# Transforms along a row as four 64x64 quarters of the array instead of block-diagonal pairs

## Chip, cores and metric

The kernel runs on one core of a Trainium2 chip. The metric is the device time of one execution in microseconds, and a program is judged by the median of several runs.

## What is computed

A 48 x 48 image with 768 channels passes through four layers, one after the other: a transformer block with relative-position attention and an MLP, a spectral layer, a scan layer (a recurrence of 12 steps with a 3x3 convolution), and a second spectral layer. The change concerns the spectral layers and the output of the scan layer. Cut to what matters, a spectral layer is

```python
xs = jnp.fft.rfft2(x, axes=(1, 2))               # rows h, then 25 frequencies along w
# per frequency and block of 96 channels: complex 96x96 layer, relu, complex 96x96 layer
o1 = relu(complex_mul(xs, w1) + b1)
o2 = complex_mul(o1, w2) + b2
out = jnp.fft.irfft2(softshrink(o2, 0.01), s=(48, 48), axes=(1, 2)) + x
```

and the scan layer ends with `silu(h @ W_out + b_out)`. All numbers are 32-bit floats.

## The kernel before

The two-dimensional transform is made as two products with small cosine and sine matrices. The channels are worked in two halves of 384 (`TB`), and the 24 pairs of image rows (two rows of 48 points, 96 partitions) in six groups of four pairs.

**Forward along w** is `spectrum_rows`. One product takes a pair of rows: the stationary matrix `fw` is 96 x 112 and block-diagonal, one block of cosines and sines for each of the two rows, and the 384 channels of the half are the moving columns. A group has four such products, each into a PSUM tile of its own. ScalarE and VectorE empty the tiles in turn (`Evac`, lines 63 and 65), and one DMA writes the group to `yu`, a spectrum in DRAM of 112 lines (frequency, real or imaginary part, row of the pair) by 24 pairs.

**Mixing** is `spectrum_mix`. For each half, each of five chunks of five frequencies, and each of four blocks of 96 channels it runs a software pipeline of four stages: the transform along h (L1559), the first complex layer (L1573 to L1575), the second (L1594, L1595) and the transform back along h (L1609). It loads `yt` from `yu` and stores `us` back into the same places. Other work is put into its steps by a function `beside`.

**Back along w** exists in two forms. In layer 1 (`afno_first`, L1696) the spectrum is the stationary operand and `iw` the moving one, because the scan layer needs channels on partitions. In layer 3 (`afno_second`, L1792) `iw`, 100 x 96 and block-diagonal, is stationary and 384 channels move; VectorE adds the product to `x3` (L1794), and one DMA on ScalarE's queue stores a group of four pairs (L1798). The last group is stored pair by pair on two queues (L1796). The group's spectrum, `gt`, is loaded by one DMA on SyncE's queue (L1784).

Where this work stands:

- The forward transforms of layer 1 run inside the MLP (`afno_follow`). Of twelve groups eleven are put between the MLP's products (L960, L1023), with a PSUM pool of only two tiles; the twelfth runs in the mix of layer 1, with eight.
- The forward transforms of layer 3 run inside the output of the scan layer. There, L1365 makes two rows' 384 output channels, VectorE adds the bias into a temporary `st` (L1367), and ScalarE writes Silu of it into `x3` (L1368), which has 96 partitions by 24 pairs by 768 channels. Every two pairs of row pairs the generator yields, and `afno_second` puts a forward group in (records `so_f`). Both share a pool of six PSUM tiles.
- Of the twelve groups back of layer 3, the six of half 0 are put into the steps of the mix (the table `backs`), and those of half 1 come after its end. For half 1 the lines of the first four chunks are loaded early (`most`), and the lines of the last chunk when its `us` has been stored (`rest`).

The order on each engine is that of the program, as a scheduler of the framework settles it when the kernel is built; each engine then works its list in order and waits on semaphores. The constants are made in `shape_constants`.

Of the kernel before, what the change touches and what calls it, by code (L numbers as in the profile page):

```python
# [20 lines left out]
P = 128  # L21
# [24 lines left out]
YR = 112  # L46
# [1047 lines left out]
def scan_phase(tc, ident, w, wts, rows_back, xh, x_close, c_d, cr_d, out_open):  # L1094
# [18 lines left out]
    K = 112  # L1113
# [5 lines left out]
    with tc.tile_pool(name="sc_s", bufs=1, side="left") as sp:  # L1119
# [3 lines left out]
        def out_weights():  # L1123
            wp = out_open("so_w")
            wo = wp.tile([P, 2, C], F32, tag="wo", name="wo")
            nc.sync.dma_start(wo, wo_d)
            return wo, load_bcast(nc, wp, bo_d, C, "bo", parts=BS)
# [203 lines left out]
        x3 = out_open("x3").tile([BS, NPR, C], F32, tag="x3", name="x3")  # L1331
        hg = s[ITERS % 2].rearrange("p n r t -> p (n r t)").rearrange("p (t n) -> p t n", t=NPR)
        with (
# [11 lines left out]
            def turned(j, q4):  # L1345
# [4 lines left out]
                hTs[j, q4] = tp.tile([P, 4, 2, G], F32, tag=f"hT{j}_{q4}", name=f"hT_{j}_{q4}", bufs=1)  # L1350
                nc.scalar.copy(hTs[j, q4], ps.rearrange("p (i s w) -> p i s w", i=4, s=2)[:, :, :, :G])
# [4 lines left out]
            for half in range(2):  # L1356
                cols = slice(half * TB, (half + 1) * TB)
                for p2 in range(NPR // 2):
                    if half == 0 and p2 % 2 == 0:
                        turned(1, p2 // 2)  # L1360
                    for t in range(2):
                        pr = 2 * p2 + t
                        ps = psum(f"{pr}_{half}")
                        for j in range(2):
                            nc.tensor.matmul(ps[:BS, :TB], lhsT=hTs[j, pr // 4][:, pr % 4].rearrange("p s w -> p (s w)"), rhs=wo[:, j, cols], start=j == 0, stop=j == 1)  # L1365
                        t_ = tp.tile([BS, TB], F32, tag="t", name=f"st_{pr}_{half}")
                        V.tensor_tensor(t_, ps[:BS, :TB], bo[:, cols], ALU.add)  # L1367
                        nc.scalar.activation(x3[:, pr, cols], t_, AF.Silu)  # L1368
# [16 lines left out]
def block_kernel(ctx: ExitStack, tc: tile.TileContext, a: dict):  # L1385
# [68 lines left out]
    yu = [dram.tile([YR, G // 2, TB], F32, tag=f"yu{i}", name=f"yu{i}") for i in range(2)]  # L1454
    todo = []
    follow_in = lambda *args: afno_follow(nc, xa_d, a["fw2"], yu, todo, *args)
# [29 lines left out]

def spectrum_rows(nc, fw, x, yu, half, g, psum, pool, ev, name, bufs=2):

    ys = pool.tile([YR, 4, TB], F32, tag="ys", name=f"{name}_ys_{half}_{g}", bufs=bufs)
    for i in range(4):
        ps = psum(f"f_{half}_{g}_{i}")
        nc.tensor.matmul(ps[:YR, :TB], lhsT=fw, rhs=x[:, i, :], start=True, stop=True)
        ev(ys[:, i, :], ps[:YR, :TB])
    nc.sync.dma_start(yu[half][:, 4 * g : 4 * g + 4, :], ys)


def spectrum_open(tc, stack, name, a, layer, yu, side):  # L1500
# [20 lines left out]
    def load(half, kc):  # L1521
        if (half, kc) not in yts:
            yts[half, kc] = yp.tile([BS, KC, TB], F32, tag="yt", name=f"{name}_yt_{half}_{kc}")
            nc.sync.dma_start(yts[half, kc], yu[half][4 * KC * kc : 4 * KC * (kc + 1)].rearrange("(k q) p c -> (q p) k c", q=4))
# [5 lines left out]
def spectrum_mix(tc, name, opened, yu, psum, keep, side, halves, beside):  # L1530
# [10 lines left out]
    with tc.tile_pool(name=f"{name}_s", bufs=2, side=side) as sp:  # L1541
# [61 lines left out]
        def s_ifft_h(i):  # L1603
# [12 lines left out]
            if b == HB - 1 or (last and b == HB // 2 - 1):  # L1616
                done = slice(b // 2 * 2 * BS, (b + 1) * BS) if last else slice(0, TB)
                nc.sync.dma_start(yu[half][4 * KC * kc : 4 * KC * (kc + 1), :, done].rearrange("(k q) p c -> (q p) k c", q=4), us[:, :, done])
# [11 lines left out]
def load_spectrum(nc, pool, yu, half, g, name, bufs):  # L1630
    gt = pool.tile([YR, 4, TB], F32, tag="gt", name=f"{name}_gt_{half}_{g}", bufs=bufs)
    nc.sync.dma_start(gt, yu[half][:, 4 * g : 4 * g + 4, :])
    return gt


def afno_follow(nc, xa_d, fw_d, yu, todo, pool, bufs=2):

    fw = pool.tile([BS, YR], F32, tag="fw", name="f1_fw")
    nc.sync.dma_start(fw, fw_d)
# [4 lines left out]
    def load(half, g):  # L1644
        cols = slice(half * TB, (half + 1) * TB)
        xt = pool.tile([BS, 4, TB], F32, tag="x1", name=f"f1_x_{half}_{g}", bufs=bufs)
        for s in range(2):
            nc.sync.dma_start(xt[s * G : (s + 1) * G], xv[g, s, :, :, cols])
# [21 lines left out]
def afno_first(tc, a, yu, xh, rp, follow_in, load_next):  # L1670
# [10 lines left out]
    iw = rp.tile([4 * KW, BS], F32, tag="iw", name="f1_iw")  # L1681
# [9 lines left out]
    def back(half, g, dst, psum):  # L1691
        gt = gts.pop((half, g))
        for ct in range(HC):
            ps = psum(f"w_{half}_{g}_{ct}")
            for i in range(4):
                nc.tensor.matmul(ps[:, i * BS : (i + 1) * BS], lhsT=gt[: 4 * KW, i, ct * P : (ct + 1) * P], rhs=iw, start=True, stop=True)  # L1696
            ev(in_rows(dst)[:, ct, :, :G], ps[:, :TB].rearrange("p (h w) -> p h w", w=G))

    with (
# [14 lines left out]
        def beside(step):  # L1714
# [3 lines left out]
            elif step == 8:  # L1718
                nc.sync.dma_start(iw, a["iw"])
# [22 lines left out]
def afno_second(tc, a, scan, yu):  # L1742
# [7 lines left out]
    out = a["out"].rearrange("(p t) c -> t p c", t=BS)  # L1750
    x3, scan_psum = next(scan)
    with ExitStack() as stack:
        opened = spectrum_open(tc, stack, "f3", a, "L3", yu, "right")
        gp = stack.enter_context(tc.tile_pool(name="f3_g", bufs=1, side="right"))
        fw = gp.tile([BS, YR], F32, tag="fw", name="f3_fw")
        nc.sync.dma_start(fw, a["fw2"])
# [178 lines left out]
```

## Time and profile before

| | us |
|---|---|
| median of 3 runs | 3694.07 (3691.95 to 3695.59) |
| profiled execution, its own time | 3694.35 |
| its span | 3692.6 |
| MLP, from 1690 to 2705 us of the span | 1015 |
| mix and back of layer 1, 2705 to 2914 | 209 |
| scan layer, 2914 to 3358 | 444 |
| scan output with forward transform of layer 3, 3358 to 3456 | 98 |
| mix of layer 3 with back of half 0, 3456 to 3660 | 204 |
| end: back of half 1, 3660 to 3693 | 33 |

The profile is that of one execution. Engines: PE is the matrix engine (PEld its weight loads), DVE VectorE, ACT ScalarE, POOL GpSimd, SP SyncE; a q behind a name is the engine's issuing side, DMA issues above all. L1495 is line 1495 of the kernel before. A matmul in 32-bit floats appears as two records. A shape such as 96*112 96x384 is partitions times columns of the stationary operand, then those of the moving one. In the timeline a row is a start, a length, an engine, a line, names of what is written and read, and the number of merged records; the bracket at its end is the idle time before it and what ended it. The end of a matmul record is modelled, so its starts are the better clock.

### The profile page before, as it was taken

Reading aid. Unit: us, or ns where it says so; the run is one execution under the profiler, and the core shown is the slowest. Engines: PE = TensorE matmul, PEld = TensorE weight load, DVE = VectorE, ACT = ScalarE, POOL = GpSimd, SP = SyncE. Lnnn points to the kernel's source line nnn. Section 1 sums busy time; section 2 is a strip of 40 time slices with the busy share of each in tenths; the row PEclk is TensorE's granted clock in tenths of the full one; section 3 lists DMA queues with packets and bytes.
Section 4 is the critical chain, followed back from the end, with each engine's and each line's share of the span. In section 5 each row is a group of like instructions: output and inputs, shape, how many; then the busy total and the mean of one; then the engine's idle time right before and its main releaser. Section 6 shows DMA issues by size and latency. Waiting matters only on the chain.

```text
span 3692.6 us, 52195 instructions
## 1 busy us (share of the span) xinstructions
PE 3592.4 (97%) x20914; PEld 2182.6 (59%) x20914; DVE 1995.3 (54%) x3011; ACT 1140.1 (31%) x1731; POOL 666.3 (18%) x498
## 2 busy tenths in 40 slices
PE   7999989999999999999999999999999998999998
PEld 4666554444444444455555555555568867995685
DVE  6544346666666666655334323232345478994445
ACT  1222134444444444303201210121023265223341
POOL 4010001111111111051000000000023303981131
PEclk9999999999999999999999999999999999999999
DMA  7666764746554543344335433533544302112345
GB/s 254 209 219 191 220 191 127 203 125 160 140 145 118 147 121 102 88 141 157 104 122 171 128 105 121 165 105 107 155 134 111 97 20 101 37 30 83 99 121 154
DMA packets 267738, 491.82 MB, mean 133 GB/s; under 512 B 37182, under 2 KB 220286, under 8 KB 261280
## 3 DMA queue, kind: packets, MB, share of 16 engines
q1 hardware_dynamic: 257680, 467.45, 43.0%
q10 hardware_dynamic: 9808, 20.94, 1.6%
q8 instruction: 168, 2.75, 0.3%
q14 instruction: 82, 0.67, 0.1%
HBM read 344.69 MB, written 143.62 MB: 132 GB/s over the span
## 4 chain that ended last, share of the span: by engine, by line
PE 76%; DVE 3%; POOL 2%; DMA 2%; ACT 1%; issue 1%; ACTq 0%; SPq 0%; DVEq 0%; POOLq 0%
PE p L960 13%; PE p L1023 13%; PE s L623 12%; PE av L654 12%; PE c L1187 4%; PE s L633 3%; PE pj L169 3%; PE f_z L1594 2%; PE f_z L1595 2%; PE f_x L1559 2%; PE so L1365 2%; PE f_u L1609 2%; POOL t L1288 1%; DVE s L1300 1%; DVE H L1284 1%
## 5 line engine op out<-in xcount | busy, mean ns | idle before, releaser
L643 DVE TENSOR_TENSOR acc<-acc,p 128x928 f32<-128x928 f32 (+1 forms) x480 | 565.2, 1177 | 255.2 <-ACT p L635 222.4
L635 ACT ACTIVATE p<-s 128x928 f32<-128x928 f32 (+1 forms) x540 | 506.7, 940 | 522.8 <-PE s L633 501.2
L623 PE MATMUL s<-qt,kv 64*128 64x464 f32 (+1 forms) x2160 | 529.2, 566 | 4.9 <-DMA qt<-q_d 4.9
L1023 PE MATMUL p<-w,h 128*128 128x384 f32 x1512 | 492.7, 486 | 0.0
L654 PE MATMUL av<-p,kv 128*64 128x464 f32 (+1 forms) x2160 | 456.5, 558 | 0.0
L1023 PEld LDWEIGHTS p<-w,h 128*128 128x128 f32 x1512 | 286.2, 190 | 196.9
L633 PE MATMUL s<-bt,oneh 64*128 64x464 f32 (+1 forms) x1080 | 399.1, 729 | 0.9 <-DMA bt<-rh_d 0.9
L623 PEld LDWEIGHTS s<-qt,kv 64*128 64x128 f32 x2160 | 195.4, 187 | 208.0 <-issue 201.7
L960 PE MATMUL p<-x2nT,w 128*128 128x384 f32 x864 | 293.6, 489 | 3.4 <-issue 3.4
L654 PEld LDWEIGHTS av<-p,kv 128*64 128x64 f32 x2160 | 141.9, 137 | 260.5 <-issue 256.7
L355 PE MATMUL qk<-xnT,wqk 128*128 128x384 f32 x756 | 254.0, 493 | 9.2 <-DMA wqk<-wqk_d 9.2
L1280 PE MATMUL c<-H,bands 128*48 128x96 f32 x5632 | 244.0, 247 | 11.4 <-issue 11.0
L1280 PEld LDWEIGHTS c<-H,bands 128*48 128x48 f32 x5632 | 234.4, 123 | 21.2 <-issue 11.4
L960 PEld LDWEIGHTS p<-x2nT,w 128*128 128x128 f32 x864 | 165.3, 191 | 119.3 <-issue 6.0
L960 PE MATMUL p<-xT,w 128*128 128x384 f32 x648 | 220.7, 486 | 0.0
L355 PEld LDWEIGHTS qk<-xnT,wqk 128*128 128x128 f32 x756 | 145.3, 194 | 104.8 <-issue 11.0
L999 POOL TENSOR_TENSOR rr<-rr,ml_b 128x1152 f32<-128x1152 f32 x12 | 33.3, 2776 | 953.6 <-DMA rr<-xr_d 433.0
L955 ACT ACTIVATE h<-h,ml_b 128x384 f32<-128x384 f32 x144 | 88.3, 614 | 346.2 <-DVE h L975 174.3
L1288 POOL TENSOR_TENSOR t<-s,c 128x768 f32<-128x768 f32 x80 | 144.6, 1832 | 182.5 <-DMA bands<-in_bands_dram 171.9
L960 PEld LDWEIGHTS p<-xT,w 128*128 128x128 f32 x648 | 123.1, 190 | 85.9
L633 PEld LDWEIGHTS s<-bt,oneh 64*128 64x128 f32 x1080 | 106.2, 187 | 106.0 <-issue 100.6
L1594 PE MATMUL f_z<-f_w,f_o 97*96 97x96 f32 x800 | 134.5, 250 | 0.0
(323 smaller groups left out, 4677.4 us busy)
## 6 DMA issues: line engine op xcount, KB each, us to landing
w<-w1s_d SPq DMA_DIRECT2D x36, 768.0 KB, 4.2
w<-w2s_d SPq DMA_DIRECT2D x36, 768.0 KB, 4.4
w<-w1s_d SPq DMA_DIRECT2D x36, 576.0 KB, 3.8
w<-in_mlp_w_dram SPq DMA_DIRECT2D x27, 768.0 KB, 4.5
wqk<-wqk_d SPq DMA_DIRECT2D x12, 1344.0 KB, 6.7
yu<-f_ys SPq DMA_DIRECT2D x24, 672.0 KB, 3.8
f_yt<-yu SPq DMA_DIRECT2D x20, 720.0 KB, 6.8
yu<-f_us SPq DMA_DIRECT2D x18, 720.0 KB, 4.5
```

What stands on the lines that cost most here:

```text
L355: nc.tensor.matmul(p[:, :TB], lhsT=w[:, n, c, :], rhs=ops[sb][n][:, c, :], start=c == 0, stop=c == NC2 - 1)
L623: nc.tensor.matmul(ps[:, s, :n], lhsT=keys[pr % 2][rows, kt * P : (kt + 1) * P], rhs=held(c)[rows, :n], start=True, stop=False)
L633: nc.tensor.matmul(ps[:, s, :n], lhsT=oneh[rows, b % 2, :], rhs=bts[b // 2][rows, j, :n], start=False, stop=True)
L635: nc.scalar.activation(p, ps[:, :, :n], AF.Exp)
L643: nc.vector.tensor_tensor(probs[c], probs[c], p, ALU.add)
L654: nc.tensor.matmul(avs[c][rows, : size(c)], lhsT=vals[pr % 2][:, kt, rows], rhs=p[:, s, :], start=kt == 0, stop=kt == NT - 1)
L960: nc.tensor.matmul(p[:, :TB], lhsT=w[n][:, c, :], rhs=rhs[n][:, c, :], start=c == 0, stop=c == NC2 - 1)
L1023: nc.tensor.matmul(ps[t][:, :TB], lhsT=hs[left, f][:, t * P : (t + 1) * P], rhs=wt[:, f % KW2, :], start=f == 0, stop=f == NF2 - 1)
L1187: nc.tensor.matmul(ps[:K, i, :n], lhsT=v[:, c, tok : tok + K], rhs=w[:, cc, c0 : c0 + n], start=cc == NC - 1, stop=cc == 0)
L1280: nc.tensor.matmul(ps[r0 : r0 + G, k // 4, cols], lhsT=bands[:, n - GC, i, :] if gr else bands0[:, n, i, :], rhs=H[:, n, :, d : d + NPR], ...
L1288: GP.tensor_tensor(t, sc[:, ch], c1[:, m0 : m0 + GC].unsqueeze(2).to_broadcast([P, GC, RR, NPR]), ALU.mult)
L1594: nc.tensor.matmul(out, lhsT=o1[:, j, 1:3, :].rearrange("c r h -> c (r h)"), rhs=w2t[:, b, 0, :], start=True, stop=False)
```

## The change

A row of the image gets a 64 x 64 quarter of the array instead of half of a block-diagonal matrix. The operands lie accordingly: two rows at partitions 0 to 47 and 64 to 111, each with its own matrix `fw` (48 x 64) or `iw` (50 x 64) on the same partitions, loaded twice by `by_rows`. In a forward group four quarter products (`a`: partition half of the input row, `b`: partition half of the output) fill two PSUM tiles, and a group has two such sets. Number, place and engine of the evictions stay, now with 128 partitions for 112.

The spectrum in DRAM becomes 64 lines (50 used) by 48 rows; its store and its load take two DMAs per group instead of one, its rows come in another order (the row order of `fh` and `ih` is adapted), and the load in layer 3 takes only the 50 used lines. Layer 1's back transform keeps its form with another constant (`iw2`) and a strided output. In layer 3's back transform four quarter products fill the tiles of two row pairs.

In the scan output, x3 has 112 partitions with a gap between the two rows, so the product has 112 columns, the sum with the bias goes straight into `x3`, and Silu works in place. Each store of the output becomes two. The core of the diff:

```diff
-    ys = pool.tile([YR, 4, TB], F32, tag="ys", name=f"{name}_ys_{half}_{g}", bufs=bufs)
-    for i in range(4):
-        ps = psum(f"f_{half}_{g}_{i}")
-        nc.tensor.matmul(ps[:YR, :TB], lhsT=fw, rhs=x[:, i, :], start=True, stop=True)
-        ev(ys[:, i, :], ps[:YR, :TB])
-    nc.sync.dma_start(yu[half][:, 4 * g : 4 * g + 4, :], ys)
+    ys = pool.tile([P, 2, 2, TB], F32, tag="ys", name=f"{name}_ys_{half}_{g}", bufs=bufs)
+    for j in range(2):
+        ps = [psum(f"f_{half}_{g}_{j}_{a}") for a in range(2)]
+        for a in range(2):
+            keep = slice(a * HD, a * HD + G)
+            for b in range(2):
+                nc.tensor.matmul(ps[a][b * HD : (b + 1) * HD, :TB], lhsT=fw[keep], rhs=x[keep, 2 * j + b, :], start=True, stop=True)
+        for a in range(2):
+            ev(ys[:, j, a, :], ps[a][:, :TB])
+    for b in range(2):
+        nc.sync.dma_start(pairs_of(yu[half], b, g), ys[b * HD : (b + 1) * HD].rearrange("p j a c -> p (j a) c"))
+
+def pairs_of(yu, b, g):
+    n = b * (G // 2) + 4 * g
+    return yu[:, n : n + 4, :]
...
-    yu = [dram.tile([YR, G // 2, TB], F32, tag=f"yu{i}", name=f"yu{i}") for i in range(2)]
+    yu = [dram.tile([HD, G, TB], F32, tag=f"yu{i}", name=f"yu{i}") for i in range(2)]
...
-                nc.tensor.matmul(ps[:, i * BS : (i + 1) * BS], lhsT=gt[: 4 * KW, i, ct * P : (ct + 1) * P], rhs=iw, start=True, stop=True)
+                nc.tensor.matmul(rows[:, i // 2, i % 2], lhsT=gt[:, i, ct * P : (ct + 1) * P], rhs=iw, start=True, stop=True)
...
-                            nc.tensor.matmul(ps[:BS, :TB], lhsT=hTs[j, pr // 4][:, pr % 4].rearrange("p s w -> p (s w)"), rhs=wo[:, j, cols], start=j == 0, stop=j == 1)
-                        t_ = tp.tile([BS, TB], F32, tag="t", name=f"st_{pr}_{half}")
-                        V.tensor_tensor(t_, ps[:BS, :TB], bo[:, cols], ALU.add)
-                        nc.scalar.activation(x3[:, pr, cols], t_, AF.Silu)
+                            nc.tensor.matmul(ps[:K, :TB], lhsT=hTs[j, pr // 4][:, pr % 4], rhs=wo[:, j, cols], start=j == 0, stop=j == 1)
+                        V.tensor_tensor(x3[:, pr, cols], ps[:K, :TB], bo[:, cols], ALU.add)
+                        nc.scalar.activation(x3[:, pr, cols], x3[:, pr, cols], AF.Silu)
...
-            nc.sync.dma_start(gts[half, g][rows], yu[half][rows, 4 * g : 4 * g + 4, :])
+            for b in range(2):
+                nc.sync.dma_start(gts[half, g][b * HD + rows.start : b * HD + rows.stop], pairs_of(yu[half][rows], b, g))
+
+        def store(queue, prs, cols):
+            for s in range(2):
+                queue.dma_start(out[s, :, prs, cols], x3[s * HD : s * HD + G, prs, cols])
...
-            for i in range(4):
-                ps = psum(f"w_{half}_{g}_{i}")
-                nc.tensor.matmul(ps[:BS, :TB], lhsT=iw, rhs=gt[: 4 * KW, i, :], start=True, stop=True)
-                dst = x3[:, 4 * g + i, cols]
-                nc.vector.tensor_tensor(dst, ps[:BS, :TB], dst, ALU.add)
-                if last:
-                    (nc.scalar, nc.sync)[i % 2].dma_start(out[:, 4 * g + i, cols], dst)
+            for j in range(2):
+                ps = [psum(f"w_{half}_{g}_{j}_{b}") for b in range(2)]
+                for b in range(2):
+                    keep = slice(b * HD, b * HD + KR)
+                    for s in range(2):
+                        nc.tensor.matmul(ps[b][s * HD : (s + 1) * HD, :TB], lhsT=iw[keep], rhs=gt[keep, 2 * j + s, :], start=True, stop=True)
+                for b in range(2):
+                    pr = 4 * g + 2 * j + b
+                    dst = x3[:, pr, cols]
+                    nc.vector.tensor_tensor(dst, ps[b][: HD + G, :TB], dst, ALU.add)
+                    if last:
+                        store((nc.scalar, nc.sync)[b], slice(pr, pr + 1), cols)
             if not last:
-                nc.scalar.dma_start(out[:, 4 * g : 4 * g + 4, cols], x3[:, 4 * g : 4 * g + 4, cols])
+                store(nc.scalar, slice(4 * g, 4 * g + 4), cols)
```

When the two programs are built, the scheduler keeps the order of the transforms in the MLP and the scan output: in the MLP the first three products of a group (now the first three tiles) come together, then one matmul of the MLP, then the fourth. It moves a few things elsewhere: loads of `yt` stand later on SyncE's queue, and five products of the scan layer now come before the first back transform of layer 1's second half.

## The prediction

> **What bounds the kernel now.** I read the engine table first, then the windows by stage, then the timeline around each edited line. The page:
>
> ```profile
> PE 3592.4 (97%) x20914; PEld 2182.6 (59%) x20914; DVE 1995.3 (54%) x3011; ACT 1140.1 (31%) x1731; POOL 666.3 (18%) x498
> ```
>
> TensorE is busy 97% of the span, so what leaves its path shortens the run, if no wait takes its place. The stages with edited lines, by windows (columns: length, then busy us of PE, PEld, DVE, ACT, POOL, granted clock, DMA share, GB/s):
>
> ```profile
> 1690.00:2705.00 1015.00, 1015.00 (x3182) 596.08 (x3182) 332.26 (x659) 148.70 (x255) 30.63 (x13) 1.00 0.42 129
> 3358.00:3456.00 98.00, 96.86 (x315) 50.15 (x314) 40.94 (x75) 39.59 (x81) 3.58 (x2) 0.99 0.36 105
> 3600.00:3660.00 60.00, 60.00 (x423) 45.32 (x422) 35.14 (x68) 18.18 (x43) 14.00 (x19) 1.00 0.43 124
> 3660.00:3693.00 33.00, 18.63 (x52) 8.71 (x50) 14.94 (x28) 0.00 (x0) 0.00 (x0) 0.81 0.71 205
> ```
>
> MLP, scan output and the mix of layer 3 are PE from end to end, with DVE and ACT at half or less. The last 33 us are not: loads, PE, DVE and stores follow one another.
>
> How one group of four tiles looks, in the timeline of the scan output and of the MLP:
>
> ```profile
> 3439.04 2.75 PE L1495 MATMUL so_f<-x,f_fw 96*112 96x384 f32 x8
> 3441.62 5.33 PE L1365 MATMUL so<-wo,hT 128*96 128x384 f32 x16
> ...
> 1937.21 2.32 PE L1495 MATMUL f_f<-f_x,f_fw 96*112 96x384 f32 x6
> 1938.63 0.27 PEld L1495 LDWEIGHTS f_f<-f_x,f_fw 96*112 96x112 f32 x2 [0.60 <-ACT f_ys L63]
> ```
>
> A matmul of the program is two records. 3441.62 less 3439.04 is 2.58 us for 8, so 0.322 us each: the price of 384 moving columns. In the MLP the third tile waits for ACT to empty the first (two PSUM tiles there), so a group takes 3.45 us with one MLP matmul (0.645) inside, 2.8 net.
>
> Do tiles of the array run side by side? The attention's `av` uses two 64-column halves in turn:
>
> ```profile
> 1079.73 2.56 PE L654 MATMUL av<-p,kv 128*64 128x464 f32 x12
> ```
>
> One after another, twelve would need 12 x 0.322 x 464/384 = 4.67 us; they take 2.5. The starts of single records come in pairs 7 ns apart, 0.389 us from pair to pair, and the first pair is already one of each half. Two tiles are thus shown; four at once are not.
>
> **What the Trainium skill says.** "TensorE: Matmul & The Clock Gate", Part 3, measures 6.32x for nine and 10.6x for sixteen small tiles at once, a few ns per tile: the pairs agree, no run here shows four. "TensorEngine Tiling (Array Packing)", Key Properties: changing the tiling mode drains TensorE. The trace agrees: the last `av` pair to the next L623 pair is 0.48 us instead of 0.389, and from L203 (96 columns, full array) to L623 0.178 where 96 columns need 0.080. I take 0.10 us a switch. Same page, Gotcha 1: different row tiles need different PSUM banks; the change gives each its own, so no clash is priced in. "DMA: Bandwidth & Descriptors", How many engines: a load spreads over the largest k up to 16 that divides its outer size. So 112, 80 and 32 lines use 16 engines, the new 50, 40 and 10 lines use 10; the trace has no such load to check on.
>
> **The change, part by part.** A group keeps its four PSUM tiles and four evictions; its four matmuls (8 records) become eight quarter matmuls (16 records). If four quarters run together, that is 16/4 x 0.322 = 1.29 us plus two switches, 0.20: 1.49 instead of 2.58, a gain of 1.09 where PE is the path.
>
> 1. Scan output, so_f, 12 groups. The cover: between two groups run 5.16 us of L1365. A group needs rows that ended 2.58 us earlier; the chain from their last record is 0.56 to the DVE start, 0.55, 0.04, ACT 0.52, 0.05 = 1.72. DVE has 4 x 0.55 + 2 x 0.56 = 3.3 and ACT about 3.6 of the new period of 6.65, so neither becomes the bound. Eleven groups gain 12.0; after the twelfth the mix waits for the last evictions (PE starts 3.89 us after its first record), of which I give 1.2. **-13.2**. Writing x3 directly and Silu in place, 112 rows for 96, 112 weight columns for 96 and the hT copy of 448 elements for 384 (0.48 to about 0.53) hide under PE; uncovered they would cost under 0.1 us each.
>
> 2. Layer 3 back, half 0, six groups inside the PE-bound mix (2.58 each): 6 x 1.09 = **-6.5**. Of the step's 6.1 us, DVE uses 4.6. The output store becomes two issues on ACT's queue (0.32 each, waiting for the four adds); behind it stands the copy of L1578, which in the trace follows 2.4 us later. No charge.
>
> 3. MLP, eleven groups. Tiles one and two now stream together, but the third still waits for the first's eviction: switch 0.10, second record at 0.42, ACT from 0.985 (0.564 after the record, as in the trace) to 1.46, third tile 1.51 to 2.25 (with the 0.1 of a cold restart), switch, MLP matmul to 3.0, switch, fourth tile 3.1 to 3.74 on a half-used array, switch: 3.84 against 3.45. **+0.39 x 11 = +4.3**. With free switches it is zero, with 0.15 each +6.5. The transform moves to quarters, but the wait replaces the stream. The store that follows becomes two on SP (0.31 each) and starts about 0.4 later; behind it stand weight loads with four buffers, some 20 us ahead.
>
> 4. Layer 1's last group in the mix, eight banks: 2.60 to 1.49, **-1.1**.
>
> 5. Handovers through DRAM. From MLP to mix, PE's idle 1.5 us at 2705.5 follows the yu store and yt load: one more issue plus item 3's lateness, **+0.7**. The spectrum loads at 2914 become pairs (+0.35), but the scheduler now puts five scan products that don't need them first: 0, between -1 and +1. The yt and us transfers move the same 96 rows of 1536 B; the order of yt_1 and yt_2 behind xa_d and f_x leaves over 10 us to their use. The inverse of layer 1 (L1696) keeps its matmuls and only strides its output: 0.
>
> 6. The end. Now:
>
> ```profile
> 3670.08 17.44 PE L1792 MATMUL f_w<-f_gt,f_iw 100*96 100x384 f32 x48 [8.90 <-DMA f_gt<-yu]
> 3674.01 14.10 DVE L1794 TENSOR_TENSOR x<-f_w,x 96x384 f32<-96x384 f32 x22 [0.50 <-PE f_w L1792]
> ```
>
> PE feeds one tile each 0.645 us and DVE follows at 0.641. With quarters PE would need 7.8, so DVE's own pace decides: three queued adds took 1.47 us in the mix, 0.49 each. First add 1.6 after the start, 24 x 0.49, about 0.2 of early hunger: 13.6 for 18.07, -4.4. Against it: the second load of the first tile +0.35, and the last row stored by two DMAs, +0.65 with the wait of one queue. The new 10-engine loads and 3.54 MB of stores meet in less time; the window 3679 to 3685 has DMA already at 319 GB/s and 0.96 busy, so some comes back: **-3.3**, from -1 to -5.
>
> Sum: -13.2 - 6.5 + 4.3 - 1.1 + 0.7 - 3.3 = -19.1. The profiled execution took 3694.35 (span 3692.6 and 1.75 around it), 0.28 over the median of 3694.07. So **3675 us**.
>
> **Rivals.**
>
> Only two quarters at a time (12%). Each matmul is two records of one tile. If the second blocks the queue, two tiles overlap, as all pairs in the trace would also allow. For it: no case of four in the trace. Against it: the first pair in `av` is already one of each half, so the other half's first record passed the waiting second one. A group then streams 2.58 plus 0.20: 0.2 x 19 + 4.3 + 0.7 + 0.7 at the end = +9.5, **3703.6**. It turns at about 2.1 us a group, two and a half quarters at a time: above that the run is slower.
>
> Gains half taken back (15%). Four run together, but bursts of four banks make so_f or the next L1365 wait for evictions, some 0.5 us a group (6), and the end stays DMA-bound (2.3): -10.8, **3683**. For it: so_f shares six banks with L1365. Against: DVE and ACT half idle.
>
> Switches hide and the MLP groups don't lose (15%): +0 instead of +4.3, 0.1 less in each other group: -25, **3669**.
>
> The change doesn't reach PE at all (3%): a stage reordered by the scheduler costs more than it gains; 3690 to 3698.
>
> **Numbers.** The main case has 55%. A measurement of this kernel can tell about 0.2%, 7.4 us, from no change. Faster by more than that: the main case, the third and most of the second, 0.82; same 0.09 (rest of the second and the last); slower 0.09, the first rival less its milder half. The main case alone spans 3670 to 3681 (switch 0.05 to 0.15, end -1 to -5); with the two neighbours 3666 to 3688.
>
> **What would show it.** Right: the 16 records of so_f and of the back in about 1.3 us, the four first ones within tens of ns; L1365 0.1 late behind them; the MLP groups at 3.8 us with one MLP matmul inside; the scan output stage 13 us shorter; DVE back to back at 0.49 at the end. Wrong: 2.6 us for 16 records, or PE idle before L1365 with DVE or ACT as releaser.

## The result and the profile after

The changed kernel takes 3690.83 us in the median of 12 runs (3686.57 to 3696.45), the kernel before 3693.4 in as many beside it: the ratio is 0.9994, with a 95% interval of 0.9985 to 1.0002. That is no change that can be measured. The forecast was 3675 us, with a chance of 0.82 for faster. The profiled execution took 3690.74, its span 3688.8.

The engine table of the page after:

```profile
PE 3573.8 (97%) x21202; PEld 2157.4 (58%) x21202; DVE 1993.9 (54%) x3011; ACT 1140.2 (31%) x1731; POOL 666.8 (18%) x498
```

PE has 18.6 us less to do (3592.4 before), but the span is only 3.8 shorter. The work left TensorE's list; the time was lost elsewhere. The windows by stage (columns as before: length, busy us of PE, PEld, DVE, ACT, POOL, clock, DMA share, GB/s):

```profile
1690.00:2705.00 1015.00, 1008.37 (x3244) 582.05 (x3244) 331.06 (x656) 148.63 (x255) 30.61 (x12) 1.00 0.43 129
3358.00:3456.00 98.00, 92.47 (x438) 46.09 (x439) 44.33 (x79) 43.02 (x87) 4.36 (x4) 0.95 0.53 133
3600.00:3653.00 53.00, 51.69 (x445) 38.15 (x443) 32.92 (x67) 17.10 (x39) 12.60 (x17) 1.00 0.44 124
...
3669.00:3681.00 12.00, 4.76 (x54) 2.28 (x45) 6.77 (x15) 0.00 (x0) 0.00 (x0) 0.78 0.94 271
3681.00:3688.80 7.80, 2.82 (x12) 0.85 (x12) 1.58 (x3) 0.00 (x0) 0.00 (x0) 0.50 0.40 117
```

and, in the kernel before, the end's fullest twelve microseconds:

```profile
3677.00:3689.00 12.00, 10.52 (x33) 5.05 (x31) 9.56 (x18) 0.00 (x0) 0.00 (x0) 1.00 0.93 295
```

In the MLP, PE was busy for all of 1015.00 us before and now has gaps of 6.6 us in the same window. In the end PE works for 7.6 of the last 19.8 us, at a clock down to 0.50, while the DMA share is 0.94 and then 0.40: an end full of transfers, and behind it a wait. Before, PE worked for 10.5 of twelve microseconds beside as full a DMA.

Read from the starts of the same records in both traces, the stages moved as in the table. The record f_u, a mark in it, is the transform back along h (L1609 before, L1626 after).

| stage, from mark to mark | before | after | moved | forecast |
|---|---|---|---|---|
| start to the MLP's first product (L98, a transpose) | 1677.2 | 1678.0 | +0.9 | 0 |
| MLP, from there to the mix's first transform along h | 1029.9 | 1038.4 | +8.5 | +5.0 (items 3 and part of 5) |
| layer 1's mix and the scan layer, to the first L1365 | 648.5 | 644.6 | -3.9 | -1.1 |
| scan output, to the first transform back along h | 115.9 | 106.9 | -9.0 | -13.2 |
| rest of layer 3's mix, with half 0 back | 189.8 | 185.4 | -4.4 | -6.5 |
| the end, from the last record of f_u to the span's end | 31.4 | 35.4 | +4.0 | -3.3 |

Four stages fell short: the MLP by 3.5 us, the scan output by 4.2, the mix by 2.1, the end by 7.3. Each figure is of one profile, so it matters how far a stage varies over the runs below that do not edit it. The scan output takes 106.7 to 107.7 us, layer 3's mix repeats to 0.01, and the end takes 35.4 to 36.2. The MLP takes 1037.3 to 1041.7, so its shortfall is at least 2.4. The third row is not shown to be an effect of the change: it takes 642.9 to 645.9 in the runs of the changed kernel with an unedited MLP, and e11, where the code of this stage is that of the kernel before, takes 645.9 as well.

**The quarters.** One group of the scan output in the timeline:

```profile
3409.32 0.49 PE L1365 MATMUL so<-wo,hT 128*112 128x384 f32 x1
3409.73 1.52 PE L1505 MATMUL so_f<-x,fw 48*64 48x384 f32 x16
3411.18 1.22 PE L1365 MATMUL so<-wo,hT 128*112 128x384 f32 x3
```

Sixteen records take 1.45 us. Single starts in them are at 0.00, 0.01, 0.01, 0.02, then 0.37 to 0.39, 0.70 to 0.72, 1.02 to 1.04: four at a time, 7 ns apart. The Trainium skill ("TensorE: Matmul & The Clock Gate", Part 3) has small tiles of the array start about 4 ns apart; the trace agrees in kind. The two-at-a-time rival is dead. But the switch is dearer than the 0.20 us I put in: 0.41 instead of 0.32 from the last full matmul into the quarters, 0.05 more from the first quad to the second, 0.41 out of them, and 0.41 from the first full matmul behind to the second. A group costs 1.64 us over the matmuls around it, for 1.49 forecast.

The same in the MLP, a group before and one after:

```profile
1937.21 2.32 PE L1495 MATMUL f_f<-f_x,f_fw 96*112 96x384 f32 x6
1939.37 0.81 PE L1023 MATMUL p<-w,h 128*128 128x384 f32 x2
1940.02 0.81 PE L1495 MATMUL f_f<-f_x,f_fw 96*112 96x384 f32 x2
1940.66 3.71 PE L1023 MATMUL p<-w,h 128*128 128x384 f32 x11
...
2015.55 0.49 PE L1023 MATMUL p<-w,h 128*128 128x384 f32 x1
2015.96 0.88 PE L1505 MATMUL f_f<-f_x,fw 48*64 48x384 f32 x8
2017.40 0.86 PE L1505 MATMUL f_f<-f_x,fw 48*64 48x384 f32 x4 [0.57 <-ACT f_ys L63]
2018.19 0.91 PE L1023 MATMUL p<-w,h 128*128 128x384 f32 x2
2019.04 0.86 PE L1505 MATMUL f_f<-f_x,fw 48*64 48x384 f32 x4
2019.83 1.56 PE L1023 MATMUL p<-w,h 128*128 128x384 f32 x4
```

After the change come eight records, a wait of 0.57 for ScalarE to empty the first bank, four records, one matmul of the MLP, and four more: the sequence is the forecast one. Its price isn't. Net of the MLP's own matmuls the eleven groups cost 3.42 to 3.47 us each, against 2.76 to 2.81 before. From group to group the start drifts by 0.66 us against before (1.64 at the first, 2.30 at the second, 2.95 at the third, 8.30 at the eleventh).

**The mix.** Of the six groups of half 0, four bring 0.96 to 1.04 us each. The last two bring 0.25. The timeline of one of these, cut to what matters, before and after:

```profile
3657.63 2.75 PE L1792 MATMUL f_w<-f_gt,f_iw 100*96 100x384 f32 x8
...
3658.96 0.64 DVE L1600 TENSOR_TENSOR f_Z<-f_z,f_cl 96x480 f32<-96x480 f32 x1
...
3660.22 0.97 PE L1609 MATMUL f_u<-f_Z,f_ih 96*96 96x480 f32 x2
```

```profile
3645.36 1.52 PE L1816 MATMUL f_w<-f_gt,iw 50*64 50x384 f32 x16
3645.47 0.65 DVE L1615 TENSOR_SCALAR f_cl<-f_z 96x480 f32<-96x480 f32 x1 [0.81 <-PE f_z L1612]
...
3646.28 0.56 DVE L1820 TENSOR_TENSOR x<-f_w,x 112x384 f32<-112x384 f32 x1
3646.75 0.64 DVE L1617 TENSOR_TENSOR f_Z<-f_z,f_cl 96x480 f32<-96x480 f32 x1
3647.31 1.47 DVE L1820 TENSOR_TENSOR x<-f_w,x 112x384 f32<-112x384 f32 x3
...
3647.54 1.02 PE L1626 MATMUL f_u<-f_Z,f_ih 96*96 96x480 f32 x2 [0.66 <-DVE f_Z L1617]
```

VectorE makes `f_Z`, the operand of L1626, behind an add of the group. Before, the group itself (2.58 us) covered that; the quarters (1.45) don't, and PE waits 0.66.

**The end.** The chain that ended last, before, from the last store of the mix on (start, length, what):

```profile
3661.94 5.09 DMA yu<-f_us
...
3667.09 2.86 DMA f_gt<-yu
...
3670.08 17.46 PE f_w L1792 x48
```

and after:

```profile
3654.24 6.43 DMA yu<-f_us
...
3660.72 2.34 DMA f_gt<-yu
...
3663.20 5.40 PE f_w L1816 x30
...
3668.62 2.91 DVE x L1820 x7
3671.53 4.91 DMA out_dram<-x
...
3676.46 5.23 DMA f_gt<-yu
...
3681.83 2.84 PE f_w L1816 x12
```

Before, PE's 17.46 us are the end. After, an output store stands between VectorE's adds and the load of the last tile, though the load reads nothing that the store writes, nor fills its buffer. SyncE's own waits in this stretch (total us, times, longest):

```profile
SPq L1801 <- DMA out_dram<-x: 8.9, 2, 7.3
```

In the trace's records a DMA issue of SyncE or ScalarE, or the waiting instruction just before it, waits on the very semaphore that it will raise; eight semaphores (101 to 106, 108 and 109) serve the loads and stores of both queues. The second half of the last load, issued at 3676.46, 7.6 us after the first half, waits on the one that the store of 3671.53 had taken, thus for that store to land. PE then does its last twelve records at half clock (2.84 us).

### The profile page after: what moved, and what is told of

It reads as the page before. It is cut to its first block, busy times and chain, and to the rows that moved or that the text cites. A ratio compares the mean times of both kernels' runs of the same rounds, so it can differ in the third digit from the quotient of the medians.

```text
span 3688.8 us, 52870 instructions
## 1 busy us (share of the span) xinstructions
PE 3573.8 (97%) x21202; PEld 2157.4 (58%) x21202; DVE 1993.9 (54%) x3011; ACT 1140.2 (31%) x1731; POOL 666.8 (18%) x498
## 4 chain that ended last, share of the span: by engine, by line
PE 74%; DVE 3%; POOL 3%; DMA 2%; issue 2%; ACT 2%; SPq 0%; ACTq 0%; POOLq 0%; DVEq 0%
PE p L960 13%; PE p L1023 13%; PE s L623 12%; PE av L654 12%; PE c L1187 4%; PE s L633 3%; PE pj L169 2%; POOL t L1288 2%; PE f_z L1611 2%; PE f_z L1612 2%; PE f_x L1576 2%; PE so L1365 2%; PE f_u L1626 2%; PE f_o L1590 1%; DVE s L1300 1%
## 5 line engine op out<-in xcount | busy, mean ns | idle before, releaser
L1280 PEld LDWEIGHTS c<-H,bands 128*48 128x48 f32 x5632 | 235.4, 124 | 19.6 <-issue 11.3
L355 PEld LDWEIGHTS qk<-xnT,wqk 128*128 128x128 f32 x756 | 144.8, 193 | 104.8 <-issue 10.1
L633 PEld LDWEIGHTS s<-bt,oneh 64*128 64x128 f32 x1080 | 106.4, 188 | 107.7 <-issue 101.2
L169 PE MATMUL v<-wv,xnT 128*128 128x384 f32 x378 | 133.0, 497 | 0.6 <-DVE xnT L144 0.5
```

What stands on the lines that cost most here:

```text
L169: nc.tensor.matmul(p[:, :TB], lhsT=rhs[n][:, c, t * P : (t + 1) * P], rhs=w[:, c, :], start=c == 0, stop=c == NC2 - 1)
L355: nc.tensor.matmul(p[:, :TB], lhsT=w[:, n, c, :], rhs=ops[sb][n][:, c, :], start=c == 0, stop=c == NC2 - 1)
L633: nc.tensor.matmul(ps[:, s, :n], lhsT=oneh[rows, b % 2, :], rhs=bts[b // 2][rows, j, :n], start=False, stop=True)
L1280: nc.tensor.matmul(ps[r0 : r0 + G, k // 4, cols], lhsT=bands[:, n - GC, i, :] if gr else bands0[:, n, i, :], rhs=H[:, n, :, d : d + NPR], ...
```

## The experiments

All ratios are to the kernel before, run on the same chip beside them; its medians lay between 3692.9 and 3694.8, so the ratios are to be compared and not the medians. Two kernels whose intervals overlap are not told apart by time. The last three columns are of one profile each. "The end" is from the last record of f_u to the end of the span. In e1's expectation "31 us" is from that record to PE's last (31.3).

| kernel | median us | ratio (95%) | end | of it, to half 1's first store | first store to end |
|---|---|---|---|---|---|
| before | 3693.40 | 1 | 31.4 | 14.1 | 17.3 |
| changed kernel | 3690.83 | 0.9994 (0.9985 to 1.0002) | 35.4 | 13.8 | 21.6 |
| e1, last load early | 3694.30 | 0.9997 (0.9989 to 1.0006) | 36.1 | 13.9 | 22.3 |
| e2, stores on POOL | 3690.45 | 0.9989 (0.9980 to 0.9997) | 33.9 | 14.2 | 19.6 |
| e3, MLP full array | 3684.90 | 0.9974 (0.9963 to 0.9984) | 35.6 | 13.9 | 21.7 |
| e4, four banks | 3675.47 | 0.9949 (0.9935 to 0.9962) | 36.2 | 14.1 | 22.1 |
| e5, loads ahead | 3692.97 | 0.9999 (0.9991 to 1.0008) | 36.0 | 18.6 | 17.4 |
| e6, e5 and e4 | 3674.53 | 0.9947 (0.9933 to 0.9960) | 36.0 | 18.5 | 17.5 |
| e7, e2 with two groups' stores out | 3687.61 | 0.9978 (0.9969 to 0.9988) | 30.5 | 13.6 | 16.9 |
| e8, scan output full array | 3703.79 | 1.0023 (1.0015 to 1.0030) | 35.6 | 13.9 | 21.7 |
| e9, fewer stores | 3695.84 | 1.0007 (0.9998 to 1.0015) | 37.2 | 14.1 | 23.1 |
| e10, e9 and e4 | 3676.87 | 0.9953 (0.9940 to 0.9967) | 38.6 | 14.5 | 24.1 |
| e11, before with transfers doubled | 3697.68 | 1.0014 (1.0004 to 1.0023) | 34.1 | 16.0 | 18.1 |
| e12, e2 and e4 | 3672.41 | 0.9942 (0.9928 to 0.9955) | 33.3 | 14.9 | 18.4 |

### The MLP: undone, and with four banks

```diff
# e3, in afno_follow, in place of spectrum_rows
...
+        for i in range(4):
+            ps = psum(f"f1_f_{half}_{g}_{i}")
+            nc.tensor.matmul(ps[:, :TB], lhsT=fw, rhs=xts[half][:, i, :], start=True, stop=True)
+            ev(ys[:, i, :], ps[:, :TB])
...
# e4, in mlp_phase
         def psum(name):
+            if name.endswith(("_1_0", "_1_1")):
+                return pm.tile([P, 512], F32, tag="m", name=name)
             return pt.tile([P, 512], F32, tag="t", name=name)
```

In e3 `fw` is 96 x 128 and block-diagonal, and the rows of `x1` lie close together again.

> The changed kernel, but layer 1's forward transform (eleven groups beside the MLP, one in the mix) as four full-array matmuls each with a block-diagonal weight of 96 by 128, stored to the new DRAM layout by four transfers instead of two. Theory: each MLP group of the changed kernel costs 0.66 us more than before (its start drifts by that much from group to group against before), since its third and fourth matmul sets wait for a PSUM bank and each burst pays a switch of the array; undone, eleven groups give 7.3 back, and the group in the mix takes 1 to 2 of it: about 3685 where before takes 3693, the stage from 1690 to the last L1023 as long as before (1015.5 us). Rival: the drift comes from the loads and stores around the transform, which this keeps or doubles: no change, 3690.

Measured: 3684.9, and the MLP's stage of the table 1031.4 us (changed kernel 1038.4, before 1029.9). That is 7.0 for the 7.3 expected, from a stage that varies by 4. Clearer are the starts of the groups: against before they no longer drift (0.75 us behind at the second group, 0.86 at the eleventh). The drift was the transforms.

> The changed kernel, but in the MLP the second pair of each group's four PSUM tiles comes from the six banks of the products instead of the two banks that all four shared. Theory: the third set of quarters then needn't wait for ScalarE to empty the first bank; a group costs what it does in the scan output, 1.64 us over the foreign matmuls around it instead of 3.46, so the MLP is 11 x 1.8 = 20 us shorter: about 3671 where before takes 3693. Rival: the products need their six banks (three in use, three being emptied), and L1023 or L960 waits for the evictions of f_ys instead, some 1 us a group: 3680 to 3685, with idle PE named on ScalarE or VectorE at those lines.

Measured: 3675.5, 4 us above the figure expected, and the stage 1018.3 us, 20.1 less than in the changed kernel. A group in its timeline:

```profile
2014.12 0.49 PE L1025 MATMUL p<-w,h 128*128 128x384 f32 x1
2014.53 1.52 PE L1507 MATMUL f_f<-f_x,fw 48*64 48x384 f32 x16
2015.98 1.24 PE L1025 MATMUL p<-w,h 128*128 128x384 f32 x3
```

It is the scan output's group: 1.45 us, no wait. No product of the MLP waits for an eviction in this trace, so the rival falls. The same quarters that lost 0.66 us a group with two banks win 1.13 (2.77 less 1.64) with four. By the ratios the whole run gains 16.6 us of the 20.1. Part is lost again behind the MLP: from the mix to the first L1365 the four kernels with four banks need 646.1 to 648.5 us, those with two banks 642.9 to 645.9. Why was not tried.

### The scan output undone

```diff
-            spectrum_rows(nc, fw, x3[:, 4 * g : 4 * g + 4, half * TB : (half + 1) * TB], yu, half, g, psum, gp, ev, "f3")
+            for i in range(4):
+                nc.tensor.matmul(ps[:, :TB], lhsT=fw, rhs=x3[:, 4 * g + i, half * TB : (half + 1) * TB], start=True, stop=True)
+                ev(ys[:, i, :], ps[:, :TB])
...
```

> The changed kernel, but layer 3's forward transform, beside the scan output, as four full-array matmuls with a block-diagonal weight of 112 by 128, stored by four transfers. Measured theory: a group in quarters costs 1.64 us over the matmuls around it (0.09 more into the first quad, 0.37, 0.31 and 0.33 between quads, 0.41 to the next full matmul and 0.10 more to the one after) against 2.58, so eleven groups lose 10.4 us and the last 0 to 1: 3700 to 3702, the stretch from the first L1365 to the first L1626 of the mix longer by 9 to 11 us. The price in the prediction (1.49 a group and 1.2 for the last) would give 13, 3704. Rival (the evictions or the new x3 layout set this stage's pace, not PE): under 5 us.

Measured: 3703.8, a ratio 0.0029 or 10.7 us above the changed kernel's, and the stretch 118.0 us for 106.9. The time alone is too coarse to tell 10.4 from 13. The stretch, 10.4 to 11.3 longer than in the runs that leave it alone, fits the measured price and not the forecast's, and the rival falls. The stretch is also 2.2 above before's 115.9. That is not the groups, for from the first to the eleventh they take 79.2 us for 79.5. Of the 2.2, 1.9 lie between the mix's first transform along h and its first back; this piece takes 16.1 to 17.4 us in the other runs of the changed kernel, 17.5 here and 15.6 before. Its cause was not looked for.

### The end: order, semaphores, bytes

```diff
# e1
-            if (half, g) not in gts:
+            if (half, g) == (1, NTB - 1):
+                gts[half, g] = gp.tile([P, 4, TB], F32, tag="ys", name="f3_gt_last", bufs=2)
+            elif (half, g) not in gts:
...
+        load(1, NTB - 1)
         for g in range(NTB):
             back(1, g)
-            if g == 0:
-                load(1, NTB - 1)
# e2
-                store(nc.scalar, slice(4 * g, 4 * g + 4), cols)
+                store(nc.gpsimd if half else nc.scalar, slice(4 * g, 4 * g + 4), cols)
```

> The changed kernel, but the last tile of the last back transform (half 1, group 5) is loaded into a sixth buffer (one of the two used by the forward transform, free by then), its two transfers issued ahead of the last half's stores. Theory A (the changed end is late because the second transfer of that load is issued only when a store that stands eight transfers earlier has landed): PE has its 16 records in one go behind group 4, the span from the last L1626 to the end falls from about 31 us to 23, and the run is 8 us under the changed kernel, about 3683 where before takes 3693. Rival B (the end is bound by the DMA engines: the same bytes, and loads of 40, 10 and 50 lines that use fewer engines, have to pass whatever their order): the stores take the wait that the load had, the end stays at 30 to 31 us and the run at 3690.

Measured: nothing gained, and the end 36.1. The rival's outcome came true, but not for its reason. Even ahead of all stores on its own queue, the load's second transfer was issued at 3676.09, when a store issued at 3671.16 had landed 4.91 later. A place on SyncE's list does not help a transfer that shares a semaphore with one on ScalarE's.

> The changed kernel, but the ten output stores of the last half's groups 0 to 4 are issued on GpSimd's queue instead of ScalarE's; the last tile keeps its buffer and its place in the program. Theory A1 (the loads on SyncE's queue and the stores on ScalarE's take the same few completion semaphores in turn, so that twice as many transfers make the second half of the last load wait for a store to land): its second transfer follows the first within 0.5 us, not 7.6, and the end is 5 to 7 us shorter: about 3685 where before takes 3693. Theory A2 (what is late is the buffer: the load waits for group 0's matmuls): the first transfer is issued at the same place, 5.6 us after the end's first matmul, and nothing is gained beyond 1 us. Rival B (DMA engines full): no gain, 3690, the second transfer issued early and landing as late as now.

Measured: 3690.45, the end 33.9. GpSimd's stores have semaphores of their own (116 to 123 in the trace), and the two transfers of the last load go out together:

```profile
3668.28 0.65 SPq L1801 DMA_DIRECT2D f_gt<-yu  x2
```

PE's last record comes 22.9 us after f_u instead of 31.3. So A1's mechanism is shown; but of 8.4 us only 1.5 reach the end, which the time (0.9989 for 0.9994) cannot resolve. One more thing differs: on GpSimd's queue the same stores go in packets of 4608 bytes, on ScalarE's in packets of 1536. From the first store on, packets keep a DMA engine busy for 3.40 us per MB that the sixteen move together, for 3.47 in the changed kernel, so little of the gain can lie there. The windows of this run tell why so little is left:

```profile
3670.00:3682.00 12.00, 7.17 (x70) 3.67 (x62) 8.76 (x19) 0.00 (x0) 5.14 (x9) 0.78 0.99 291
3682.00:3688.80 6.80, 0.00 (x0) 0.00 (x0) 0.00 (x0) 0.00 (x0) 0.00 (x0) 0.50 0.39 116
```

The DMA engines are busy for 0.99 of twelve microseconds, and nothing computes in the last 6.8. VectorE does what the prediction asked of it: on the chain of this trace fourteen adds run back to back in 6.62 us, 0.47 each, and the end hardly shortens. Is it bytes? e7 leaves out the stores of two of the half's six groups.

```diff
-            if not last:
+            if not last and (half, g) not in ((1, 2), (1, 3)):
```

> The kernel with the last half's stores on GpSimd's queue, but the stores of groups 2 and 3 of that half (four transfers, 1.18 MB, a third of the last half's output) are left out. Theory D (DMA-bound end): 640 packets less of 1536 B are 3.2 to 4 us of all 16 engines; the end, 33.9 us with all stores, falls to 30 or less: about 3686 where before takes 3693. Rival (the end is a chain of latencies: issue, landing, last adds, last stores): the end stays within 1 us of 33.9 and the time at 3690.

Measured: the end is 30.5, 3.4 shorter than in e2; the ratio, 0.0011 lower, is too coarse to tell. Of the 3.4, 0.6 lie ahead of the first store, where nothing was edited. From the first store on the stretch is 2.7 us shorter (16.9 for 19.6), somewhat less than the 3.2 to 4 expected. The stores left out were 256 packets of 4608 bytes, not 640 of 1536, and the time that packets took there fell by as much: from 15.1 to 12.3 us per DMA engine. So theory D holds for this kernel: from the first store on the DMA engines set the pace. Four transfers went with the bytes; the two were not separated.

```diff
# e5
...
-        for g in range(NTB - 1):
-            if g > 2:
-                load(1, g, most)
+        for g in (3, 4, 5):
+            load(1, g, most)
+        for g in range(NTB):
             load(1, g, rest)
         for g in range(NTB):
             back(1, g)
-            if g == 0:
-                load(1, NTB - 1)
```

> The changed kernel, but all loads of the last half (the 40-line parts of tiles 3, 4 and 5, then the 10-line parts of all six) are issued ahead of the first store of that half, tile 5 into a sixth buffer that the forward transform has left. Theory D (from the first store on, the DMA engines are the bound: 2112 store packets of 1536 B at about 80 ns on 16 engines are 10.5 us, and some 3 us of loads of tiles 4 and 5 lie among them; PE's pace is of no account): the 3 us of loads move into the stretch before, where the DMA share is 0.3 to 0.5, and the time from the end of the last L1626 to the end of the span falls from 35.4 us (31.4 before the change) to 29 or 30: about 3685 where before takes 3693. Theory A (only the late issue of the last tile's second load): the same order of gain, 5 to 7 us, but PE's last record then at least 6 us earlier and DMA idle after it. Rival: twelve more small issues on SyncE wait for one another's landing and PE's first matmul of the end comes later by 2 us or more: no gain, 3690.

Measured: no gain, 3693, end 36.0, and both theory D and the rival are in it. With all loads ahead, PE's last record comes 25.4 us after f_u, and from the first store to the end it takes 17.4 us, 4.2 less. (The stores are 2304 packets, not 2112.) But PE starts 4.9 us later. The first small load is issued 7.3 us after f_u, as in the changed kernel, but five loads of 40 lines stand just ahead of it: it lands after 7.4 us instead of 2.3, and PE starts at that moment. The small loads behind it wait for earlier loads to land, as the rival had it; SyncE's issues:

```profile
3663.40 9.27 SPq L1803 DMA_DIRECT2D f_gt<-yu  x10
```

These ten issues take 9.27 us. Moved loads pay at the front what they save behind.

> The run before with four PSUM banks for the MLP's groups added (second pair from the products' six): the two gains lie in different stages and add: 18.8 us from the MLP and what the loads ahead give alone, 4 to 7. 3668 to 3671 where before takes 3693. If the end gains nothing, 3675.

Measured: 3674.5, the case without a gain at the end.

### The end: the number of transfers

```diff
# e9
-                    if last:
-                        store((nc.scalar, nc.sync)[b], slice(pr, pr + 1), cols)
-            if not last:
-                store(nc.scalar, slice(4 * g, 4 * g + 4), cols)
+                if last:
+                    store((nc.scalar, nc.sync)[j], slice(4 * g + 2 * j, 4 * g + 2 * j + 2), cols)
+            if not last and (half == 0 or g % 2 == 0):
+                store(nc.scalar, slice(4 * (g - 1) if half and g else 4 * g, 4 * g + 4), cols)
# e11, in the kernel before: each load and store cut in two by lines, for example
+                for r in (slice(0, G), slice(G, BS)):
+                    nc.scalar.dma_start(out[r, 4 * g : 4 * g + 4, cols], x3[r, 4 * g : 4 * g + 4, cols])
```

> The changed kernel, but the last half's stores as 10 transfers instead of 18, of the same bytes: group 0 alone, groups 1 and 2 together, 3 and 4 together, and the last tile in two pairs of rows. Theory A (number of transfers: each issue waits for the transfer that took the same one of eight semaphores eight issues before, so twice the transfers keep half the bytes in flight and hold the last load back): the second transfer of the last load is issued within 3 us of the first instead of 7.6, PE's last record comes 4 us earlier, and the stretch from the end of the last L1626 to the end of the span falls from 35.4 us to 31 or 32: about 3687 where before takes 3693. Theory D (bytes on full DMA engines alone): the same bytes take the same time, the larger stores start later: 35 to 37 us, 3690 to 3692.

Measured: the end 37.2, longer by 1.0 than any unedited one; in time, 1.0007, it is not told apart from the kernel before. The last load's two transfers do go out 0.32 us apart, as theory A said, but PE's last record comes no earlier. The chain of this run:

```profile
3671.04 4.22 DMA out_dram<-x
3675.26 0.02 issue
3675.28 0.27 SPq L1801
```

Now it is the load of tile 4 that gets the semaphore of group 0's store and waits for it, PE with it. The number of stores alone doesn't decide; who follows whom on the eight semaphores does. Theory A fails in this form.

> The kernel before, its transforms unchanged, but every load of layer 3's back transform and every store of its output cut in two by lines (80 as 48 and 32, 32 as 16 and 16, 112 as 64 and 48, stores of 96 as 48 and 48): twice the transfers, the same bytes, line counts that are all multiples of 16. Theory A (number of transfers): the end, 31.4 us from the last L1609 to the end of the span, grows to 34 or 35, with PE waiting for the last load as in the changed kernel: 3696 to 3697 where before takes 3693. Theory D or the loads on fewer engines (what costs is bytes, or the 50, 40 and 10 lines of the changed kernel): the end stays within 1 us of 31.4, 3693 to 3694.

Measured: 3697.7 (1.5 to 8.5 us more than before, by the interval), and the end grows by 2.7 to 34.1, with full-array transforms, line counts that are multiples of 16, and the same bytes. PE did not wait for the last load, as theory A had it; the chain is longer at its front:

```profile
3658.69 6.23 DMA yu<-f_us
...
3665.35 2.93 DMA f_gt<-yu
...
3668.41 17.81 PE f_w L1794 x48
```

PE starts 1.6 us later after f_u than before, the first store goes out 1.9 later, and from there to the end it takes 0.8 more. The cut transfers cost by themselves. That the changed kernel's loads of 50, 40 and 10 lines use 10 engines, as the prediction drew from the Trainium skill ("DMA: Bandwidth & Descriptors", How many engines), is borne out by its trace: each of these 34 loads raises its semaphore 11 times, where every load of 112, 80 or 32 lines before raises it 16 times. What this costs no run here isolates.

> The fewer, larger stores together with four PSUM banks for the MLP's groups. The stages are apart, so the gains add: 18.8 us and what the fewer stores give alone (0 to 4): 3671 to 3675 where before takes 3693.

Measured: 3676.9, above the range and not told apart from e4; the end is 38.6. The fewer stores bring nothing here either.

> Four PSUM banks for the MLP's groups, and the last half's ten larger stores on GpSimd's queue. The MLP's gain (18.8 us in time, 20.4 in the stage) and that of the queue (the end 33.9 us instead of 35.4 to 36.2) lie apart and add: the end at 34 us, about 3672 to 3674 where before takes 3693. If the queue's gain was the spread of single profiles, the end is 35 to 36 and the time 3675.

Measured: 3672.4, ratio 0.9942, the MLP's stage 1018.6 and the end 33.3, for 36.2 in e4. In the profiles the two gains add. This is the lowest median of the study, 0.58% under the kernel before and 0.52% under the changed one (0.9942 over 0.9994); the four kernels with four banks, 0.9942 to 0.9953, are not told apart by time.

## Why the prediction was wrong

The likeliest case lay 16 us too low, and the range ended at 3688. Its mechanism was right on PE: four quarters run at once, and the groups in the MLP lose. The step that failed is item 6, the path through the end; items 1, 2 and 3 were right in kind and mis-sized. Term by term:

- **Item 1** (-13.2, measured -9.0). A group gains 0.94, not 1.09, since a round trip into quarters costs 0.35 and not 0.20. From the first group to the last the stretch is 10.1 us shorter, for 12.0. The 1.2 us given for the last group did not come: the mix starts 3.93 us after its first record, 3.89 before. Another 1.1 went ahead of the first group and behind the mix's first transform. Each of these pieces differs by over 1 us between runs that leave it alone, so the 1.1 has no shown cause.
- **Item 2** (-6.5, measured -4.4). I checked that VectorE had time for the adds, but not whom they stand ahead of: `f_Z`, in the last two groups.
- **Item 3** (+4.3, measured 0.66 x 11 = +7.3). The sequence was right; only the switches, three bursts to a group, were mis-sized. The bound with 0.15 a switch, +6.5, came close.
- **Items 4 and 5** (-1.1, +0.7). Around layer 1's last group L1626 gains 1.05 us in the changed kernel, and nothing in e3, where this group is full-array again. The handover from MLP to mix is 2.05 us for 1.53. Both are of the forecast size. The stage's further gain is not shown, as said at the table.
- **Item 6** (-3.3, measured +4.0) is the step that failed in kind. "DVE's own pace decides" was false. The 4.0 are -0.3 up to the first store and +4.3 from there. PE starts 0.9 us later than before (the second load had been priced at 0.35), and at half clock: its first two groups take 2.58 and 2.56 us, and the first group before, also at half clock, 4.38. So the first store goes out about as late as before (13.8 for 14.1). From then on what decides is the DMA: in e2 the adds run at 0.47 each and the end stays long, and in e7 it shortens as the packets' time does. I had seen the window at 0.96 busy and left 0.1 to 0.2 us of the sum for it. The 4.3 us go with the loads that lie among the stores, for e5, with every load ahead, needs 17.4 us from the first store on, and before needed 17.3. More of the loads lie there than before: from the first store on 4.61 MB move, 4.23 before, with the same stores. Of the 4.3, e2 takes back 2.0 by freeing the last load from a store's semaphore. Doubling the transfers at the same bytes, which I had priced at 1.0 for the whole end, costs 0.8 in this stretch of the kernel before (e11). If the two add, which no run shows, 1.5 us stay open. The rest of e11's 2.7 lies ahead of the first store, where the changed kernel lost nothing; so e11's 2.7 and the 1.5 that e2 takes off the end are no account of the 4.0, though their sum, 4.2, comes close.

Of the rivals, the second, gains half taken back, had the right direction and 3683. Its first reason, evictions behind bursts of four banks, was not seen: PE waits for none in the scan output. Its second, an end that stays DMA-bound, was right in kind and far too small: 2.3 us, where the end lay 7.3 above the forecast. The last rival's range, 3690 to 3698, holds the result, but by luck: its reason, a stage reordered by the scheduler, is not what the runs show.

## What to carry to other kernels

Small tiles of the array paid where a group's operands and banks let a whole burst run: in the MLP the same change lost 0.66 us a group with two PSUM banks and won 1.13 with four, so count banks and switches per burst before counting columns. Where a stage feeds stores, price the bytes from the first store to the end; a faster engine ahead of a full DMA was worth nothing here. And count transfers, not only bytes: an issue can wait for an unrelated transfer that holds its semaphore, which the chain shows as a DMA between two things that share no data.

## What was not expected of the hardware

- A round trip from full array to quarters and back costs more than the 0.10 us a side put in for it: 0.09 us in, 0.05 at the second quad, 0.09 out and 0.09 to 0.10 at the second matmul behind, 0.33 to 0.35 in all.
- In the changed kernel the granted clock fell to half 1.8 us after the mix's last record, and came back only 5.6 us after PE's first record of the end (3.5 in the kernel before, 7.0 in e2). Meanwhile 16 quarter records took 2.58 us instead of 1.29.
- In the full stretch a store of 288 KB took 4.2 (e9) and 4.9 us (changed kernel) to land from ScalarE's queue, and 5.6 to 7.5 from GpSimd's (e2). Over twelve microseconds the DMA engines moved 271 GB/s at 0.94 busy in the changed kernel, 295 at 0.93 before and 291 at 0.99 in e2.
